# Both FFN products of a two-layer transformer made of seven half-size products instead of eight (Strassen's scheme), with a block's second product behind the next block's first

## The chip, the cores and the metric

The kernel runs on one core of one Trainium2 chip. A core has a matrix engine, TensorE (PE; its loads of stationary weights are listed apart as PEld), three engines for elementwise work, VectorE (DVE), ScalarE (ACT) and GpSimd (POOL), and queues for DMA transfers, issued here from SyncE (SP) and from POOL. Each engine works through its own instructions in order and waits on semaphores for the others. PE writes to PSUM only, which has eight banks of 512 f32 values in each of 128 partitions; DVE and ACT read PSUM, POOL works in SBUF alone. The metric is the device time of the launch in microseconds (us).

## The reference

All is f32. `x` has 4 batches of 1024 rows of 256. Two layers follow each other, an attention with 16 heads of 64 and the same FFN behind each (the reference's first attention and its second differ; neither is touched here):

```python
x = x + _L0_attn_a_ref(_layernorm(x, axis=-1), kernel, WO)
x = x + _L0_ffn_ref(_layernorm(x, axis=-1), w1, b1, w2, b2)
x = x + _L0_attn_b_ref(_layernorm(x, axis=-1), ...)
x = x + _L0_ffn_ref(_layernorm(x, axis=-1), w1, b1, w2, b2)

def _L0_ffn_ref(x, w1, b1, w2, b2):
    h = jax.nn.gelu(jnp.einsum('bse,eh->bsh', x, w1) + b1, approximate=False)
    return jnp.einsum('bsh,he->bse', h, w2) + b2
```

`w1` is 256 x 1024, `w2` is 1024 x 256.

## The kernel before

The rows of `x` stay in SBUF for the whole launch, `xs[b]` for each batch. An FFN works on eight blocks of 512 rows (`QB`), two to a batch. For a block n, `normed(n)` (L390) standardizes four tiles of 128 rows on ACT into `xn` and adds b2 to `x` on POOL. `turned(n)` (L398) transposes `xn` on PE, eight transposes of 128 x 128 into two banks of the pool `ps_mm`, and ACT copies each bank to `hT` (L156). `up(n, f)` (L403), for each of eight groups of 128 of the 1024 hidden columns, makes one tile of the first product in a bank of the pool `ps_sc`: two f32 matmuls, one for each half of the 256 inputs, with `w1` stationary and 512 rows moving. ACT applies Gelu with the bias from PSUM to `gT` (L414). `down(n, t)` (L416), for each of four tiles of 128 rows, makes the second product in a bank of `ps_mm`: eight matmuls with `gT` stationary and 256 columns of `w2` moving. After every second tile DVE adds the bank to `x` (L428), and in the last FFN SP stores those rows (L430).

The profile records an f32 matmul as two passes, each with a weight load of its own.

`ps_sc` has three buffers of two banks (in the attention they hold the scores), `ps_mm` has two of one bank. The order of instructions is written out by hand and kept (`manual_schedule`); semaphores and buffer turnover come from the framework. A new tile takes the buffer that has been free longest.

`ffn_between` (L434) weaves an FFN into the launch in three parts. `ends` are pieces for the last steps of the attention before it: block 0's `normed`, `turned` and its whole `up`, block 1's `normed` and `turned`, and the first `down(0, 0)`. `rest` is the stretch of its own: the remaining `down(0, t)`, and then for each block m from 1 the eight `up(m, f)`, `turned(m + 1)` and the four `down(m, t)`. Between the ups stand small pieces: `normed(m + 1)` after f = 1; for m = 1 after f = 2 the statistics (`measure`, two DVE instructions each) of the eight tiles of blocks 6 and 7; in the first layer after f = 3 four `measure` for layer B's norm; for m = 3 after f = 4 `finish`, which makes the factors out of the statistics (an ACT Sqrt, which needs a table load, and DVE work around it). In the first layer also `prologue`, 40 pieces that prepare the first pair of heads of layer B, one after each up for m = 4 and 5 and two for m = 6 and 7. Block 7's `down` goes behind `rest`: in the first layer into the first steps of the next attention (`last`), in the second it ends the launch.

The attention's tiles share pools with the FFN: `gT` is a buffer of pool `T`, and the pools `pT` (two buffers), `p`, `qk` and `v` stand free during `rest`, but for the prologue.

Of the kernel before, what the change touches and what calls it, by code (L numbers as in the profile page):

```python
# [15 lines left out]
P = 128  # L16
# [5 lines left out]
NF = F // P  # L22
# [17 lines left out]
def hybrid_block_kernel(  # L40
# [108 lines left out]
    def transposed(dst, src, c, affine=None):  # L149

        tr = group(TQ, P)
        for t in range(TQ):
            nc.tensor.transpose(tr[:, t, :], src[:, t, ts(c, P)], ident)  # L153
        trf = tr.rearrange("p t q -> p (t q)")
        if affine is None:
            nc.scalar.copy(dst[:, c, :], trf)  # L156
        else:
            nc.scalar.activation(
                dst[:, c, :], trf, AF.Identity,
                scale=affine[0][:, c : c + 1], bias=affine[1][:, c : c + 1],  # L160
            )
# [224 lines left out]
    def ffn(rows, store):  # L386

        xn, hT, gT, po = {}, {}, {}, {}

        def normed(n):  # L390
            b, qb = blocks[n]
            xn[n] = xnp.tile([P, TQ, D], F32, tag="xn", name="xn")
            for t in range(TQ):
                xt = xs[b][:, qb * TQ + t, :]
                standardize(xn[n][:, t, :], xt, *rows.factors(n, t)[:2])
                nc.gpsimd.tensor_add(xt, xt, b2_sb)  # L396

        def turned(n):  # L398
            hT[n] = lowp.tile([P, NC, QB], F32, tag="low", name="hT")
            for c in range(NC):  # L400
                transposed(hT[n], xn[n], c)

        def up(n, f):  # L403
            if f == 0:
                gT[n] = tp.tile([P, SENT], F32, tag="T", name="gT")[
                    :, : NF * QB
                ].rearrange("p (f q) -> p f q", f=NF)
            ph = ps_sc.tile([P, QB], F32, tag="sc", name="ph")
            for c in range(NC):
                nc.tensor.matmul(  # L410
                    ph, w1_sb[:, c, ts(f, P)], hT[n][:, c, :],
                    start=(c == 0), stop=(c == NC - 1),
                )
            nc.scalar.activation(gT[n][:, f, :], ph, AF.Gelu, bias=b1_sb[:, f : f + 1])  # L414

        def down(n, t):  # L416
            b, qb = blocks[n]
            if t % 2 == 0:
                po[n] = group(2, D)
            for f in range(NF):  # L420
                nc.tensor.matmul(  # L421
                    po[n][:, t % 2, :], gT[n][:, f, ts(t, P)], w2_sb[:, f, :],
                    start=(f == 0), stop=(f == NF - 1),
                )
            if t % 2:
                t0 = qb * TQ + t - 1
                xd = xs[b][:, t0 : t0 + 2, :]
                nc.vector.tensor_add(xd, xd, po[n])  # L428
                if store:
                    nc.sync.dma_start(ov[b, :, t0 : t0 + 2, :], xd)  # L430

        return normed, turned, up, down

    def ffn_between(rows, store, n_steps, nxt=None, prologue=(), ramp=None):  # L434

        normed, turned, up, down = ffn(rows, store)
        prologue = list(prologue)
        n = n_steps
        ends = [(n - 20 + i, lambda i=i: rows.measure(i // TQ, i % TQ)) for i in range(2 * TQ)]
        ends += [(n - 2, lambda: rows.finish[0]()), (n - 2, lambda: normed(0)), (n - 1, lambda: turned(0))]
        ends += [(n - 1 + (0, 0, 0, 1, 2, 2, 3, 3)[f], lambda f=f: up(0, f)) for f in range(NF)]
        ends += [(n, lambda: normed(1))]
        ends += [(n + 1, lambda m=m, t=t: rows.measure(m, t)) for m in range(2, 6) for t in range(TQ)]
        ends += [(n + 2, lambda: rows.finish[1]()), (n + 3, lambda: turned(1)), (n + 4, lambda: down(0, 0))]

        def rest():
            for t in range(1, TQ):
                down(0, t)
            for m in range(1, len(blocks)):
                for f in range(NF):
                    up(m, f)
                    if f == 1 and m + 1 < len(blocks):
                        normed(m + 1)
                    if f == 2 and m == 1:
                        for i in range(2 * TQ):  # L460
                            rows.measure(6 + i // TQ, i % TQ)
                    if f == 3 and nxt:
                        for t in range(TQ):
                            nxt.measure(m - 1, t) if m <= 6 else None
                    if f == 4 and m == 3:
                        rows.finish[2]()
                        if nxt:
                            nxt.finish[0]()
                    for _ in range((0, 0, 0, 0, 1, 1, 2, 2)[m]):
                        if prologue:  # L470
                            prologue.pop(0)()
                if m + 1 < len(blocks):
                    turned(m + 1)
                    for t in range(TQ):
                        down(m, t)
            while prologue:
                prologue.pop(0)()
            if nxt:
                nxt.finish[1]()
            else:  # L480
                for t in range(TQ):
                    down(len(blocks) - 1, t)

        last = [(t - 1, lambda t=t: down(len(blocks) - 1, t)) for t in range(TQ)]
        if nxt:
            last += [
                (12 + 2 * i, lambda i=i: nxt.measure(6 + i // TQ, i % TQ)) for i in range(2 * TQ)
            ] + [(30, lambda: nxt.finish[2]())]
        return ends, rest, last
# [94 lines left out]
    def layer_b(rows):  # L584
# [4 lines left out]
        def batch_b(b):  # L589
            work = []  # L590
            for qb in range(NQB):
                k = {}

                def first(t, b=b, k=k, qb=qb):
                    if t == 0:
                        if b:
                            k["x1"] = xnp.tile([P, TQ, D], F32, tag="xn", name="x1")
                        else:
                            k["x1"] = ptp.tile([P, SENT], F32, tag="pT", name="x1")[
                                :, : TQ * D  # L600
                            ].rearrange("p (t d) -> p t d", t=TQ)
                    xt = xs[b][:, qb * TQ + t, :]
                    standardize(k["x1"][:, t, :], xt, *rows.factors(NQB * b + qb, t)[:2])
                    nc.gpsimd.tensor_add(xt, xt, k["x1"][:, t, :])
# [5 lines left out]
                def turned(c, b=b, k=k, qb=qb):  # L610
                    if c == 0:
                        p, tag = (highp, f"high{qb}") if b % 2 == 0 else (lowp, "low")
                        cs[b, qb] = p.tile([P, NC, QB], F32, tag=tag, name="hc")
                    transposed(cs[b, qb], k["x1"], c, affine=(lns_sb, lnb_sb))
# [141 lines left out]
```

## Time and profile before

Three runs took 3277.23, 3277.85 and 3282.06 us, median 3277.85. The profiled execution has a span of 3281.4 us.

| what | us |
|---|---|
| span of the profiled execution | 3281.4 |
| busy: PE, DVE, ACT, POOL | 3201.6, 2531.3, 2109.0, 1958.4 |
| first product (L410), PE: 512 recorded matmuls of 512 columns | 230.2 busy |
| second product (L421), PE: 1024 recorded matmuls of 256 columns | 226.0 busy |
| weight loads of L421 | 0.190 each |
| Gelu from PSUM (L414), 128 x 512 | 0.686 each |
| add from PSUM (L428), 128 x 512 on DVE | 0.687 each |
| b2 add (L396), 128 x 256 on POOL | 0.728 each |
| first layer's FFN, `down(0, 0)` to the end of `up(7, 7)` | 1453.15 to 1676.71 |
| second layer's FFN, `down(0, 0)` to the end of the last `down` | 3061.36 to 3277.35 |

How to read the lines: a group of instructions is named by its line in the kernel, its engine, the operation, and the tiles written and read; then comes how often it ran, its busy time, the mean length of one in ns, and the idle time of the engine ahead of it with what ended it. A line of the timeline has a start, a length, and instructions that follow one another merged, with their number behind an x; a bracket gives the idle time ahead and who ended it. The chain of waits follows the last instruction back to the first, at each step to what released it.

### The profile page before, as it was taken

To read this page: it belongs to the slowest core of one execution; us is meant where nothing else is said; L and a number is where in the kernel's file an instruction comes from. 1 tells how busy PE (TensorE), PEld (TensorE's weight loads), DVE (VectorE), ACT (ScalarE), POOL (GpSimd) and SP (SyncE) were. 2 spreads that over 40 slices of the span, in tenths; PEclk is the share of its full clock that TensorE was granted. 3 is DMA by queue.
4 is the path that set the end of the run, shared out by engine and by line. 5 is a ranking of instruction groups with operands and counts; after the bars stand their busy time and mean duration, and the time that the engine had idled before them with its cause. 6 is when DMAs were issued, how large, how long until landed. Compare 5 with 4: busy or idle time off the path is not lost.

```text
span 3281.4 us, 126564 instructions
## 1 busy us (share of the span) xinstructions
PE 3201.6 (98%) x52736; PEld 2022.3 (62%) x52736; DVE 2531.3 (77%) x2386; ACT 2109.0 (64%) x4304; POOL 1958.4 (60%) x2738
## 2 busy tenths in 40 slices
PE   8999999999999999999999999999999999998999
PEld 4666666666666666666555556666656666665666
DVE  7988888888888888941049889998989999998100
ACT  5666666666666666642447777777778777777332
POOL 4544454545444445430159888998989999996110
PEclk9999999999999999999999999999999999999999
DMA  8888888888888888840029889998888899998100
GB/s 226 224 220 213 226 223 222 219 227 223 222 214 218 222 229 225 218 116 0 2 81 237 223 217 240 242 240 236 240 229 240 240 243 247 245 246 214 38 20 20
DMA packets 244697, 642.13 MB, mean 196 GB/s; under 512 B 74304, under 2 KB 102976, under 8 KB 244128
## 3 DMA queue, kind: packets, MB, share of 16 engines
q1 hardware_dynamic: 161104, 397.60, 47.6%
q0 software_dynamic: 83024, 236.44, 25.8%
q8 instruction: 419, 6.86, 0.9%
q14 instruction: 150, 1.23, 0.1%
HBM read 43.39 MB, written 4.19 MB: 15 GB/s over the span
## 4 chain that ended last, share of the span: by engine, by line
PE 78%; SPq 8%; DMA 5%; DVE 3%; ACT 3%; issue 3%; POOL 1%; DVEq 0%; POOLq 0%; ACTq 0%
PE sc L238 23%; PE mm L304 21%; PE mm L167 16%; SPq L295 7%; PE mm L421 7%; PE ph L410 7%; PE mm L176 5%; DMA pT<-T 4%; DVE T L271 1%; DVE nmax L249 1%; ACT p L251 1%; PE mm L153 1%; POOL oT L316 0%; ACT gT L414 0%; SPq L214 0%
## 5 line engine op out<-in xcount | busy, mean ns | idle before, releaser
L249 DVE TENSOR_REDUCE nmax<-sc 128x1 f32<-128x1024 f32 x1024 | 1204.5, 1218 | 226.7 <-PE sc L238 223.5
L251 ACT ACTIVATE p<-sc,nmax 128x1024 f32<-128x1024 f32 x1024 | 1145.3, 1119 | 324.0 <-DVE nmax L249 324.0
L271 DVE STREAM_TRANSPOSE T<-p 128x2176 f32<-128x2176 f32 x512 | 1247.1, 2436 | 41.0 <-DMA pT<-T 17.6
L238 PE MATMUL sc<-kT,qT 64*64 64x512 f32 x8192 | 1085.5, 599 | 16.0 <-ACT p L251 10.6
L304 PEld LDWEIGHTS mm<-pT,v 64*64 64x64 f32 x32768 | 950.3, 133 | 145.6 <-issue 103.4
L304 PE MATMUL mm<-pT,v 64*64 64x128 f32 x32768 | 984.5, 269 | 14.5 <-issue 13.5
L295 POOL DMA_DIRECT2D pT<-T x1280 | 629.6, 499 | 121.1 <-PE sc L238 56.2
L316 POOL TENSOR_TENSOR oT<-oT,pT 128x256 f32<-128x256 f32 x256 | 186.1, 727 | 718.7 <-ACT oT L314 636.3
L238 PEld LDWEIGHTS sc<-kT,qT 64*64 64x64 f32 x8192 | 333.1, 133 | 409.9 <-issue 277.1
L328 POOL TENSOR_TENSOR x<-x,got 128x512 f32<-128x512 f32 x256 | 330.9, 1293 | 27.8 <-ACT got L326 23.9
L326 ACT COPY got<-mm 128x512 f32<-128x512 f32 x256 | 150.0, 586 | 283.0 <-PE mm L167 282.9
L428 DVE TENSOR_TENSOR x<-x,mm 128x512 f32<-128x512 f32 x32 | 22.0, 687 | 367.2 <-PE mm L421 367.1
L167 PE MATMUL mm<-wo,oT 128*64 128x256 f32 x2048 | 278.4, 393 | 19.6 <-POOL oT L316 18.6
L167 PEld LDWEIGHTS mm<-wo,oT 128*64 128x64 f32 x2048 | 124.6, 136 | 266.4 <-POOL oT L316 217.4
L414 ACT ACTIVATE gT<-ph,b_sb 128x512 f32<-128x512 f32 x128 | 87.5, 686 | 301.9 <-PE ph L410 301.8
L260 ACT COPY p<-total 128x128 f32<-128x128 f32 x512 | 151.8, 296 | 195.4 <-DVE total L259 188.5
L167 PE MATMUL mm<-hT,w 128*64 128x512 f32 x1024 | 242.9, 596 | 1.0 <-ACT hT L156 1.0
L421 PE MATMUL mm<-w_sb,gT 128*128 128x256 f32 x1024 | 226.0, 381 | 6.6 <-ACT hT L156 6.6
L410 PE MATMUL ph<-hT,w_sb 128*128 128x512 f32 x512 | 230.2, 603 | 0.5 <-ACT hT L156 0.5
L421 PEld LDWEIGHTS mm<-w_sb,gT 128*128 128x128 f32 x1024 | 193.1, 190 | 39.4 <-ACT hT L156 9.4
L396 POOL TENSOR_TENSOR x<-x,b_sb 128x256 f32<-128x256 f32 x64 | 44.5, 728 | 275.6 <-ACT xn L147 275.6
L251 ACT ACTIVATION_READ_ACCUMULATOR p<-sc,nmax 128x1 f32 x1024 | 205.3, 200 | 0.0
(90 smaller groups left out, 2473.1 us busy)
## 6 DMA issues: line engine op xcount, KB each, us to landing
pT<-T SPq DMA_DIRECT2D x2688, 136.0 KB, 4.7
pT<-T POOLq DMA_DIRECT2D x1280, 136.0 KB, 4.7
turned<-kT POOLq DMA_DIRECT2D x128, 128.0 KB, 3.5
turned<-qT POOLq DMA_DIRECT2D x128, 128.0 KB, 3.3
w<-in_wqkv_a POOLq DMA_DIRECT2D x96, 128.0 KB, 6.1
wo<-in_wo_a POOLq DMA_DIRECT2D x32, 128.0 KB, 5.4
wo<-in_wo_a POOLq DMA_DIRECT2D x64, 64.0 KB, 5.5
wo<-in_wo_b SPq DMA_DIRECT2D x32, 128.0 KB, 3.6
```

What stands on the lines that cost most here:

```text
L167: nc.tensor.matmul(out[ts(j, DH)], lhsT[:, ts(j, DH)], rhs[j], start=(first and i == 0), stop=(last and i == len(parts) - 1),)
L176: nc.tensor.matmul(out[ts(j, DH)], lhsT, rhs[:, ts(j, DH)], start=(i == 0), stop=(i == len(parts) - 1),)
L238: nc.tensor.matmul(sc[s, j][ts(half, DH), ts(m, 512)], qT()[rows, ts(2 * qs + half, DH)], kT()[rows, ts(m, 512)], start=True, stop=True,)
L249: nc.vector.tensor_reduce(nmax, sc[s, j], AX.X, ALU.max, negate=True)
L251: nc.scalar.activation(probs[s][:, :NK2, ts(j, 2), :], sc.pop((s, j)).rearrange("p (k c i) -> p k c i", c=2, i=SQ), AF.Exp, bias=nmax, acc ...
L271: nc.vector.transpose(T[h][:, :, q, :, :].rearrange("p c k i -> p k c i"), probs.pop(s))
L295: engine.dma_start(pT[h][ts(c, SQ), a], T[h][ts(a, SQ), c])
L304: nc.tensor.matmul(av[h][q][ts(j ^ q, DH)], v[ts(j, DH), k, :], pT[h][ts(j, DH), :, q, k, :], start=(k == 0), stop=(k == NK2 - 1),)
L316: nc.gpsimd.tensor_mul(parts, parts, pT.pop(h)[:, :, :, NK2, :])
L328: nc.gpsimd.tensor_add(xd, xd, got)
L410: nc.tensor.matmul(ph, w1_sb[:, c, ts(f, P)], hT[n][:, c, :], start=(c == 0), stop=(c == NC - 1),)
L421: nc.tensor.matmul(po[n][:, t % 2, :], gT[n][:, f, ts(t, P)], w2_sb[:, f, :], start=(f == 0), stop=(f == NF - 1),)
```

## The change

A product C = A B, with A, B and C cut into 2 x 2 parts, is made of seven products of parts, by Winograd's form of Strassen's scheme. Four sums are made of A's parts (`four`) and four of B's (`other`). The products are P1 = A11 B11, P2 = A12 B21, P3 = S3 B22, P4 = A22 T3, P5 = S0 T0, P6 = S1 T1 and P7 = S2 T2, and with u2 = P1 + P6 and u3 = u2 + P7 the result is C11 = P1 + P2, C12 = u2 + P5 + P3, C21 = u3 + P4, C22 = u3 + P5.

For the first product A is `w1` with its 1024 columns and 256 inputs halved, and B is `hT` with the inputs and the 512 rows halved. `up(n, f)` for f = 0 to 7 becomes two calls of `up_seven`, each for two groups of 128 columns out of either half; a product there is two f32 matmuls with 256 rows moving. For the second product A is `gT` with rows and the 1024 columns halved, B is `w2`; `down_seven` makes a whole block, eight f32 matmuls a product, with 128 columns moving. The sums of the weights are made once in each FFN (`weights`), DVE those of `w1` and POOL those of `w2`; DVE makes those of `hT` (`row_sums`), DVE and POOL those of `gT` (`act_sums`).

`seven` makes the products in the order 1, 6, 2, 7, 5, 4, 3, in five banks of `ps_sc`. P2 accumulates onto P1's bank, once ACT has copied P1 out, and P3 onto P5's, once DVE has read P5. The result that can't stand in one bank goes through SBUF. After each product a hook runs the small pieces that stood between the ups, at a place from 0 to 13 (0 to 6 in a block's first seven, 7 to 13 in its second).

A block's second product goes behind the next block's first: `down_seven(m - 1)` follows `up_seven(m, 1)`, `turned(m + 1)` and `row_sums(m + 1)`. Block 0 and block 7's `down` stay as they were. Layer B's `x1` for the first batch moves from a buffer of pool `pT` to one of pool `v`.

```diff
+        def weights():
+            wc = ptp.tile([P, SENT], F32, tag="pT", name="wc")
...
+            v = nc.vector
+            work = four([s1[:, i] for i in range(4)], w1_sb[:, 0, :m], w1_sb[:, 1, :m], w1_sb[:, 0, m:], w1_sb[:, 1, m:], [v] * 4)
+            work += other([s2[:, i] for i in range(4)], lo[:, :, :P], lo[:, :, P:], hi[:, :, :P], hi[:, :, P:], [nc.gpsimd] * 4)
+            for f in work:
+                f()
+        def row_sums(n):
+            name = ("qT", "kT")[n % 2]
+            ht[n] = qkp.tile([P, S], F32, tag=name, name="ht").rearrange("p (s q) -> p s q", s=4)
+            h = hT[n]
+            for f in other(
+                [ht[n][:, i] for i in range(4)],
+                h[:, 0, :half], h[:, 0, half:], h[:, 1, :half], h[:, 1, half:], [nc.vector] * 4,
+            ):
+                f()
+        def act_sums(n):
...
+            return four(
+                [s[:, i] for i in range(4)],
+                g[:, :hf, :half], g[:, hf:, :half], g[:, :hf, half:], g[:, hf:, half:],
+                [nc.vector, nc.vector, nc.gpsimd, nc.vector],
+            )
+        def seven(product, after, hook):
+            banks = []
+            for _ in range(3):
+                t = ps_sc.tile([P, 2, 512], F32, tag="sc", name="pw")
+                banks += [t[:, 0], t[:, 1]]
+            place = {1: 0, 6: 1, 2: 0, 7: 2, 5: 4, 4: 3, 3: 4}
+            for i, k in enumerate((1, 6, 2, 7, 5, 4, 3)):
+                bank = banks[place[k]].rearrange("p (t q) -> p t q", t=2)
+                product(bank, k, k not in (2, 3))
+                after(bank, k)
+                hook(i)
+        def up_seven(n, g, hook):
...
+            def after(bank, k):
+                if k == 1:
+                    nc.scalar.copy(x1, bank)
+                elif k == 6:
+                    nc.vector.tensor_add(u2, bank, x1)
+                elif k == 2:
+                    for t in range(2):
+                        gelu(lo[:, t, :half], bank[:, t], 2 * g + t)
+                elif k == 7:
+                    nc.vector.tensor_add(u3, bank, u2)
+                elif k == 5:
+                    nc.vector.tensor_add(hi[:, :, half:], bank, u3)
+                elif k == 4:
+                    nc.vector.tensor_add(hi[:, :, :half], bank, u3)
+                    for t in range(2):
+                        gelu(hi[:, t], hi[:, t], hf + 2 * g + t)
+                else:
+                    nc.vector.tensor_add(lo[:, :, half:], bank, u2)
+                    for t in range(2):
+                        gelu(lo[:, t, half:], lo[:, t, half:], 2 * g + t)
+        def down_seven(n, hook):
...
+            def after(bank, k):
+                bank = bank[:, :, :P]
+                if k == 1:
+                    nc.scalar.copy(x1, bank)
+                elif k == 6:
+                    nc.vector.tensor_add(u2, bank, x1)
+                    nc.gpsimd.tensor_add(x12, x12, u2)
+                elif k == 2:
+                    nc.vector.tensor_add(x11, x11, bank)
+                elif k == 7:
+                    nc.vector.tensor_add(u3, bank, u2)
+                    nc.gpsimd.tensor_add(x22, x22, u3)
+                    nc.gpsimd.tensor_add(x21, x21, u3)
+                elif k == 5:
+                    nc.vector.tensor_add(x22, x22, bank)
+                elif k == 4:
+                    nc.vector.tensor_add(x21, x21, bank)
+                    if store:
+                        nc.sync.dma_start(ov[b, :, qb * TQ + 2 : qb * TQ + 4, :], xb[:, 2:])
+                else:
+                    nc.vector.tensor_add(x12, x12, bank)
+                    if store:
+                        nc.sync.dma_start(ov[b, :, qb * TQ : qb * TQ + 2, :], xb[:, :2])
...
-        ends += [(n + 2, lambda: rows.finish[1]()), (n + 3, lambda: turned(1)), (n + 4, lambda: down(0, 0))]
+        ends += [(n + 2, lambda: rows.finish[1]()), (n + 2, weights), (n + 3, lambda: turned(1))]
+        ends += [(n + 3, lambda: row_sums(1)), (n + 4, lambda: down(0, 0))]
...
+                if m + 1 <= last:
+                    when(2, lambda m=m: normed(m + 1))
+                if m == 1:
+                    for i in range(2 * TQ):
+                        when(4, lambda i=i: rows.measure(6 + i // TQ, i % TQ))
+                if nxt and m >= 2:
+                    for t in range(TQ):
+                        when(5 + t, lambda m=m, t=t: nxt.measure(m - 2, t))
+                if m == 3:
+                    when(9, lambda: rows.finish[2]())
+                    if nxt:
+                        when(9, lambda: nxt.finish[0]())
+                if m >= 2:
+                    todo = act_sums(m - 1)
+                    for i, f in zip((3, 6, 6, 9), todo):
+                        when(i, f)
                 for f in range(NF):
...
                     for _ in range((0, 0, 0, 0, 1, 1, 2, 2)[m]):
                         if prologue:
-                            prologue.pop(0)()
...
+                            when((14 * f) // NF + 1, prologue.pop(0))
...
+                up_seven(m, 0, hook)
+                up_seven(m, 1, lambda i: hook(7 + i))
+                if m + 1 <= last:
                     turned(m + 1)
-                    for t in range(TQ):
-                        down(m, t)
+                    row_sums(m + 1)
+                if m >= 2:
+                    down_seven(m - 1, lambda i: None)
```

## The prediction

> **What bounds the kernel now.** I read the page's chain of waits first, then the chain in order of time, because the change touches two stretches only (one layer's FFN at 1453 to 1696 us, the other's at 3061 to 3277 us).
>
> ```profile
> PE sc L238 23%; PE mm L304 21%; PE mm L167 16%; SPq L295 7%; PE mm L421 7%; PE ph L410 7%; PE mm L176 5%; DMA pT<-T 4%; DVE T L271 1%; DVE nmax L249 1%; ACT p L251 1%; PE mm L153 1%; POOL oT L316 0%; ACT gT L414 0%; SPq L214 0%
> ```
>
> The two products (L410 first, L421 second) hold 14% of the chain, some 460 us. In order of time the second FFN is TensorE (PE) alone:
>
> ```profile
> 3119.43 14.08 PE mm L421 x64
> 3133.51 13.75 PE ph L410 x32
> 3148.50 14.08 PE mm L421 x64
> 3162.58 13.75 PE ph L410 x32
> ```
>
> Columns: start, length, what. A block repeats every 29.07 us (3148.50 - 3119.43). A recorded matmul is one of two passes over an f32 product, so a block has 32 passes of 512 columns and 64 of 256. The windows view says who is idle beside it:
>
> ```profile
> core 0: us, PE busy (x) PEld busy (x) DVE busy (x) ACT busy (x) POOL busy (x), PEclk, DMA share, GB/s
> 3061.36:3277.35 215.99, 213.69 (x785) 144.81 (x784) 14.84 (x34) 60.01 (x97) 17.95 (x25) 1.00 0.06 19
> ```
>
> DVE works 15 of 216 us, ACT 60, POOL 18; the clock is full. So fewer passes shorten the stretch, as long as the other engines, each working strictly in its own order, never hold PE.
>
> **PE's price list** comes from the timeline between one block's two products:
>
> ```profile
> 3234.29 1.04 PE L153 MATMUL mm<-ident,xn 128*128 128x128 f32 x8
> 3234.29 0.80 PEld L153 LDWEIGHTS mm<-ident,xn 128*128 128x128 f32 x7 [0.29 <-issue]
> ...
> 3235.07 1.07 ACT L156 COPY hT<-mm 128x512 f32<-128x512 f32 x2
> 3235.70 2.46 PEld L421 LDWEIGHTS mm<-w_sb,gT 128*128 128x128 f32 x12 [0.62 <-ACT hT L156]
> 3235.71 2.64 PE L421 MATMUL mm<-w_sb,gT 128*128 128x256 f32 x11 [0.38 <-ACT hT L156]
> ```
>
> A pass of 512 columns takes 13.75 / 32 = 0.429 us. One of 256: the eleven above start over 2.64 - 0.38 (a pass's own length) - 0.10 (the first waits for its weights) = 2.16, so 0.216 each. One of 128: eight transposes start over 1.04 - 0.27 = 0.77, seven steps of 0.110. Then 29.07 = 32 x 0.429 + 64 x 0.216 + 8 x 0.110 + a rest of 0.64, in which the second product waits for a copy out of the bank it shares with the transposes.
>
> **Gain.** First product by seven: 56 passes of 256 columns, 12.10 us in place of 13.73: -1.63. Second by seven: 112 passes of 128 columns, each with its own 128-column load. The trace has no f32 stream of that shape. Lower end 0.107 a pass (a quarter of 0.429). Upper end 0.121: a load is recorded at 190 ns, and 64-column loads at L176 last 138 ns yet come 69 ns apart in one half of the array, so 69 of the 190 overlap. I take 0.110, by the transposes and by the row at 3235.70: of its eleven steps (2.46 - 0.19 = 2.27 us) ten follow the matmuls at 0.216, which leaves 0.11 for the one free step between two f32 loads. So 12.3 in place of 13.8: -1.50; to the ends, 12 blocks x 112 x (-0.003 or +0.011) = -4 or +15. The 0.64 goes, since the seven use the other six banks. A layer has 7 first and 6 second products so made (the first block and the last block's second product stay): 7 x 1.63 + 6 x 1.50 + 6 x 0.64 = 24.3; two layers: -48.6.
>
> A rule that speaks against the change: the Trainium skill, page "TensorE: Matmul & The Clock Gate", in Part 3 under "The mechanism", says that a weight load overlaps running matmuls only if it goes to another row group. Here loads and matmuls both use all rows, and loads of 190 ns beside passes at 0.216 could not fit if they took turns; the trace disagrees. By the rule a short pass would cost 0.11 + 0.107, and the sum would rise by about 12 x 112 x 0.107 = 144 us; I don't use it.
>
> **Prices on the other engines.** DVE: 512 elements out of PSUM 0.687 (L428), 1024 at L249 1.218, hence 256 at about 0.42. A 1024-element sum from SBUF has no row: between L249's 1.218 and two L428s, 1.37; I take 1.22, the same count of elements. ACT: copy of 512 0.59, of 256 0.37; gelu of 512 0.69, so of 256 0.69 - 0.21 = 0.48; with its source in SBUF, as L608 (0.51 for 256), 0.51 and 0.72. Queued ACT work overlaps by 0.1. POOL: 0.73 for 256, 1.28 for 512, so about 2.4 for 1024. From a product's last column to DVE or ACT: 0.27 (3220.55 to 3220.82, L421 to L428); back to a streaming PE: 0.16 (a copy's end, 3235.65, to a load 0.05 later, plus 0.11).
>
> A price that hides in few instructions is two engines in SBUF at once:
>
> ```profile
> 1853.74 0.17 DVE L134 TENSOR_TENSOR b_more<-b_more,b_rstd 128x8 f32<-128x8 f32 x1
> 1853.75 1.29 POOL L659 TENSOR_TENSOR qT<-qT,turned 128x512 f32<-128x512 f32 x1
> ...
> 1854.27 0.20 DVE L136 RECIPROCAL b_more<-b_more 128x8 f32<-128x8 f32 x1 [0.37 <-ACT b_more L135]
> 1854.39 0.67 DVE L137 TENSOR_TENSOR b_shift<-b_mv,b_rstd 128x8 f32<-128x8 f32 x1
> ```
>
> L137 normally takes 0.17; begun under a POOL instruction it took 0.67 and ended 0.02 after it, while the reciprocal, with one input, ran freely. I read this as: a DVE operation with two SBUF inputs waits for the running POOL one. `act_sums` and `row_sums` are of that kind; every other new DVE add has one PSUM input.
>
> **Waits that take its place.** I follow one seven of `up_seven` (0.864 us a product, order 1, 6, 2, 7, 5, 4, 3), from its first pass, in a block with `act_sums`.
> First seven. P6 ends at 1.73; ACT copies P1 out 1.13 to 1.72, and P2, into the same bank, may run at 1.88: 0.15 lost. P7 ends 3.61; u3 on DVE to 4.56. Behind it on DVE stands the first sum (hook 3). POOL's b2 adds of the next block run from 4.43, 0.7 each, so it waits to 5.13 and ends 6.35. Only then DVE reads P5 out (to 7.04), and P3, which accumulates onto P5's bank, starts at 7.20 in place of 5.34: 1.86 lost. P3 ends 8.06, DVE's adds of P4 and P3 by 7.7 and 9.0.
> Second seven, from 8.06. The sum for hook 6 wants DVE at 9.0, but POOL's own sum (2.4) runs 8.45 to 10.87: it ends 12.1. ACT, behind four gelus, copies P1 at 9.9 to 10.5; P2 starts 10.65 in place of 9.8: 0.85. DVE then does u2 (12.8), the third sum (14.0), u3 (14.7), P5 (15.4); P3 starts at 15.55 in place of 14.1: 1.45. The whole takes 16.4, of which 4.3 PE waits, so the first product is slower than its 13.73 before. `down_seven` (1.76 us a product) hides all its copies, `row_sums` too.
> Per layer: blocks 2 to 6, 5 x 4.3 = 21.5. Block 7 has no b2 adds, and POOL's sum is early: 0.15 + 1.29 + 0.86 + 0.25 = 2.55. Block 1 has eight `measure` (4.2) at hook 4, in front of P4's read on DVE (0.53 is their pace at the ramp, 16 in 8.5 us); ACT's gelus wait for that, the copy of P1 stands behind these, and PE loses 5.7. Then comes no second product, so block 2's first waits for hT's two copies and two row sums: 2.6. Block 3's `finish` puts a wait for ACT's Sqrt (table load 1.28) in front of u3: 2.2. Sum 34.6, the second layer: 34.6 - 24.3 = +10.3.
> The first layer adds four `measure` a block on DVE, about 0.95 x 6 = 5.7, and its second `finish` in block 3, 1.8. The prologue of layer B moves too, in the same order. Its weight loads issue on an empty SP queue; its eight `change` transfers issue on POOL, now behind POOL's own sum (2.4), and their rotated tiles are wanted only after the last `down_seven` (12.3), which covers that. Up to block 7's first product this layer takes 223.6 us (1453.15 to 1676.71) against 202.2 (3061.36 to 3263.52); of the 21.4 more the view of waits gives PE's waiting 6.0 - 2.3 = 3.7, so some 17 are PE work, which now falls into the gaps of blocks 5 to 7 in part, while its ACT work lengthens others: between -10 and +5, I take -5. So 34.6 + 7.5 - 5 - 24.3 = +12.8.
> At nothing: `weights` at the first ramp (POOL is idle from 3053.2 to 3059.1, its four sums need 5.2; DVE idles 10 us) - without that cover 3 to 5 us, once a layer; the stores (two a block as before, on an empty SP queue, last one behind the same last product); x1 in another pool.
>
> **Sum:** -48.6 + 34.6 x 2 + 7.5 - 5 = +23. Against the profiled 3281.4 us that is 3304.5; the runs' median is 3277.85, so 3301.
>
> **Rivals.**
> (a) POOL and DVE don't hold each other: the walk gives 14.65 in place of 16.4, five blocks, two layers: -17.7, total +5: 3283. For it: L137 is one small instruction. Against: it and L133 (ends 0.03 behind a POOL one) agree.
> (b) Faster: the sums of `act_sums` stay off the path. Then an up loses 0.15 + 0.25 + 0.92 + 0.25 = 1.57 and the layers come to 36.6 lost against 48.6: -12, 3266. It decides if DVE is free for P5 at 4.74, with u3 done at 4.56: the sum would have to fit 0.2 us, or be taken elsewhere. Against: 1.22 is the nearest row; for it: PE's prologue work fills gaps in three blocks, and my delays are taken at their full length.
> (c) More: POOL's four adds follow one another without a gap, and the first sum gets no turn among them: it starts at 7.2 in place of 5.13, 2.1 x 10 blocks = +21, 3322; with passes at 0.121, +15 and 3316; both, 3337.
> (d) The seven don't save PE time at all, loads of 190 ns one after the other: 12 x 112 x 0.08 = +107, 3408. The free step of 0.11 is against it.
>
> **Chances.** Forecast 0.47, (a) 0.12, (b) 0.20, (c) 0.18, (d) 0.03. A measurement of this kernel can tell about 0.2% from no change (6.6 us). (b) is faster; (a) lies within; the rest is slower: 0.20, 0.11, 0.69. The range goes from (b) to between (c)'s single cases and both together: 3264 to 3332; the forecast's own, with the pass from 0.107 to 0.114, 3295 to 3310.
>
> **What would show it.** Passes: 128-column matmuls of the second product about 0.110 apart. Waits: PE idle before P3 released by DVE, before P2 by ACT; two-SBUF DVE sums longer than 1.3 under POOL; a block near 29.5 us in the second layer. Wrong, if blocks come in under 28, if PE's wait before P3 is only 0.25, or if the loads pace the second product.

## The result, and the profile after

Four runs of the changed kernel took 3373.94 to 3382.33 us, median 3375.08; four of the kernel before 3277.23 to 3288.13, median 3279.95. The ratio is 1.0283 (95% interval 1.026 to 1.0305): slower by 95 us where 23 were predicted. The profiled execution has a span of 3374.2 us against 3281.4, 92.8 more.

The page of the kernel after, busy time and the chain of waits:

```profile
PE 3203.0 (95%) x53648; PEld 2091.7 (62%) x53648; DVE 2731.1 (81%) x2674; ACT 2135.2 (63%) x4400; POOL 2035.4 (60%) x2794
...
PE 68%; SPq 12%; DVE 7%; DMA 5%; ACT 4%; issue 3%; POOL 1%; DVEq 0%; ACTq 0%; POOLq 0%
PE sc L238 19%; PE mm L304 18%; PE mm L167 14%; SPq L295 11%; PE pw L482 8%; DMA pT<-T 5%; PE mm L176 4%; DVE T L271 2%; PE mm L602 2%; DVE nmax L249 2%; ACT gT L516 1%; PE ph L591 1%; ACT p L251 1%; POOL oT L316 1%; DVE gs L410 1%
```

PE is busy as long as before (3203.0 against 3201.6) in a span 92.8 longer, so PE idles about 91 us more. The FFNs hold it. The first layer's stretch, from the first pass of `down(0, 0)` to the first of the last block's `down`, went from 226.5 to 273.5 us. The second layer's, to the end of the last `down` (as the last pass has streamed, 0.16 before its recorded end), went from 215.9 to 264.0. That is +47.0 and +48.1; the attention between them took 1382.3 against 1381.8.

The chain of the kernel after in order of time, one block of the second layer (start, length, what); L482 are the passes of all sevens:

```profile
3212.99 10.08 PE pw L482 x84
3223.15 0.59 ACT u L520
3223.78 1.15 PE pw L482 x4
3225.02 0.70 DVE u L522
3225.77 2.01 PE pw L482 x8
3227.80 0.69 DVE u L527
3228.55 1.57 issue
3230.12 0.69 DVE gT L529
3230.85 1.15 PE pw L482 x4
```

Before, two lines of PE alone made up a block. Now the chain leaves PE four times within one seven: to ACT's copy of P1 (L520), to DVE's u2 (L522) and u3 (L527), and to DVE's read of P5 (L529). PE stands in the chain as a row of short pieces.

The windows of the kernel after: first the stretch of the second layer, then a steady block, then pairs of neighbours in which the clock (PEclk) is of interest later:

```profile
core 0: us, PE busy (x) PEld busy (x) DVE busy (x) ACT busy (x) POOL busy (x), PEclk, DMA share, GB/s
3106.07:3370.18 264.11, 215.31 (x1240) 180.06 (x1240) 111.36 (x176) 73.53 (x145) 49.65 (x49) 0.96 0.05 16
...
3241.69:3275.63 33.94, 27.71 (x178) 23.46 (x177) 16.38 (x24) 10.27 (x22) 8.21 (x8) 1.00 0.05 16
...
3128.29:3131.70 3.41, 0.95 (x5) 0.49 (x3) 3.21 (x13) 0.00 (x0) 0.80 (x2) 1.00 0.00 0
3131.70:3141.90 10.20, 6.35 (x14) 4.64 (x15) 2.06 (x4) 3.44 (x7) 0.00 (x0) 0.50 0.01 2
3145.39:3148.80 3.41, 1.19 (x5) 0.73 (x5) 1.52 (x4) 2.50 (x6) 0.00 (x0) 1.00 0.00 0
3148.80:3155.60 6.80, 5.95 (x13) 4.29 (x14) 0.80 (x2) 1.81 (x5) 0.41 (x1) 0.50 0.00 0
3199.99:3203.40 3.41, 0.45 (x3) 0.04 (x1) 2.10 (x5) 2.48 (x3) 0.00 (x0) 1.00 0.00 0
3203.40:3206.80 3.40, 3.17 (x8) 2.52 (x9) 1.56 (x3) 0.34 (x1) 0.00 (x0) 0.50 0.02 5
```

No engine is full in the steady block of 33.94 us (29.07 before): DVE works 16.4 of it, ACT 10.3, POOL 8.2. The engines wait for each other in turn. The view of PE's waits in that layer says for whom (waiting engine and line, releaser, then us in total, times, longest):

```profile
PE pw L482 <- ACT u L520: 18.5, 14, 5.5
PE pw L482 <- DVE u L522: 12.1, 14, 0.9
PE pw L482 <- DVE gT L529: 6.3, 6, 1.2
PE pw L482 <- ACT u L561: 3.7, 6, 0.6
PE pw L482 <- DVE u L563: 3.5, 6, 0.6
PE pw L482 <- DVE u L527: 3.2, 1, 3.2
PE pw L482 <- ACT hT L156: 1.5, 1, 1.5
```

The prediction expected the third line and a little of the first. The copy of P1 (L520) and u2 (L522) hold PE in each of 14 sevens, and the same two steps of `down_seven` (L561, L563) in each of six. Which products wait is in the timeline, the start of one block's first seven (start, length, instructions with their number; a bracket gives the idle time ahead and who ended it). Two f32 matmuls, four recorded passes, are a product; they come as P1, P6, P2, then P7 and P5 together, P4, P3:

```profile
3222.03 1.03 PE L482 MATMUL pw<-hT,w_sb 128*128 128x256 f32 x4
...
3223.15 0.58 ACT L520 COPY u<-pw 128x512 f32<-128x512 f32 x1 [12.85 <-PE pw L482]
...
3223.78 1.13 PE L482 MATMUL pw<-ht,wc 128*128 128x256 f32 x4 [0.73 <-ACT u L520]
3225.02 0.69 DVE L522 TENSOR_TENSOR u<-pw,u 128x512 f32<-128x512 f32 x1 [2.38 <-PE pw L482]
...
3225.77 1.13 PE L482 MATMUL pw<-hT,w_sb 128*128 128x256 f32 x4 [0.85 <-DVE u L522]
...
3228.39 3.76 POOL L399 TENSOR_TENSOR x<-x,b_sb 128x256 f32<-128x256 f32 x4 [9.61 <-ACT xn L147]
3228.41 1.79 DVE L409 TENSOR_TENSOR gs<-gT 128x1024 f32<-128x1024 f32 x1
...
3230.85 1.13 PE L482 MATMUL pw<-hT,wc 128*128 128x256 f32 x4 [1.18 <-DVE gT L529]
```

P6 (3223.78) begins only when ACT has copied P1, though P6 goes into another bank (1, not 0). P2 (3225.77) begins only when DVE has read P6, though P2 goes into bank 0, which ACT freed 2 us earlier. Banks 0 and 1 are one tile of the pool. P3 (3230.85) waits for the read of P5, which stands on DVE behind the first sum of `act_sums` (L409, 1.79 us beside POOL's b2 adds, L399): that is the wait that the prediction had.

### The profile page after: what moved, and what is told of

The parts are those of the page before. It is cut to its first block, busy times and chain, and to the rows that moved or that the text cites. A ratio compares the mean times of both kernels' runs of the same rounds, so it can differ in the third digit from the quotient of the medians.

```text
span 3374.2 us, 129017 instructions
## 1 busy us (share of the span) xinstructions
PE 3203.0 (95%) x53648; PEld 2091.7 (62%) x53648; DVE 2731.1 (81%) x2674; ACT 2135.2 (63%) x4400; POOL 2035.4 (60%) x2794
## 4 chain that ended last, share of the span: by engine, by line
PE 68%; SPq 12%; DVE 7%; DMA 5%; ACT 4%; issue 3%; POOL 1%; DVEq 0%; ACTq 0%; POOLq 0%
PE sc L238 19%; PE mm L304 18%; PE mm L167 14%; SPq L295 11%; PE pw L482 8%; DMA pT<-T 5%; PE mm L176 4%; DVE T L271 2%; PE mm L602 2%; DVE nmax L249 2%; ACT gT L516 1%; PE ph L591 1%; ACT p L251 1%; POOL oT L316 1%; DVE gs L410 1%
## 5 line engine op out<-in xcount | busy, mean ns | idle before, releaser
L176 PEld LDWEIGHTS mm<-w,hT 128*64 128x64 f32 x4096 | 140.9, 138 | 71.3 <-issue 69.4
L857 POOL TENSOR_TENSOR turned<-turned,sin_sb 128x512 f32<-128x512 f32 x128 | 162.7, 1271 | 0.0
L399 POOL TENSOR_TENSOR x<-x,b_sb 128x256 f32<-128x256 f32 x64 | 54.4, 880 | 166.9 <-ACT xn L147 166.9
L287 ACT COPY pT<-T 32x1088 f32<-32x1088 f32 x128 | 140.3, 1096 | 4.6 <-DMA pT<-T 1.8
L176 PE MATMUL mm<-w,hT 128*64 128x64 f32 x4096 | 140.9, 222 | 0.2 <-ACT kT L744 0.2
L167 PE MATMUL mm<-hc,w 128*64 128x512 f32 x512 | 134.0, 601 | 0.0
```

The source lines that it names most:

```text
L167: nc.tensor.matmul(out[ts(j, DH)], lhsT[:, ts(j, DH)], rhs[j], start=(first and i == 0), stop=(last and i == len(parts) - 1),)
L176: nc.tensor.matmul(out[ts(j, DH)], lhsT, rhs[:, ts(j, DH)], start=(i == 0), stop=(i == len(parts) - 1),)
L857: nc.gpsimd.tensor_mul(other, other, sin_sb[:, ts(qb, QB)])
```

## The experiments

Ten kernels ran, each beside the kernel before on the same chip; ratios are to that kernel, with a 95% interval.

**A place of its own for each product.** The theory: PE's wait for a place in PSUM goes by the tile of two banks, so P6 waits for the reader of P1. Its rival stands below with it. The edit puts products that follow each other into different tiles and leaves the order alone:

```diff
-            place = {1: 0, 6: 1, 2: 0, 7: 2, 5: 4, 4: 3, 3: 4}
+            place = {1: 0, 6: 2, 2: 0, 7: 4, 5: 3, 4: 5, 3: 3}
```

> Only the table of banks differs: P1 and P2 in the first tile, P6, P5 and P3 in the second, P7 and P4 in the third, so that no product shares a two-bank tile with the one before it. Theory T1 (PE waits go by the two-bank tile: P6 waits for the copy of P1 out of the neighbouring bank, P2 for the read of P6): P6's wait (0.9 and 1.5 in a block's two sevens, 0.8 in the second product) and P2's for u2 (about 1.0, 0.75) go; left are P2's own wait for the copy (0.15 and about 0.85) and P3's behind the sums on DVE (1.9 and up to 1.4). Block of the second layer from 33.9 to 30 or 31 us, total 3325 to 3345. Rival R1 (the queue of DVE and ACT sets the pace, the waits only change names): block above 33, total above 3362.

Measured: 3295.68 us over ten runs, ratio 1.0027 (1.0014 to 1.004). One line of bank numbers takes back some 80 of the 95 us, more than either theory had allowed for. Its timeline, the same place of a block:

```profile
3168.43 1.03 PE L482 MATMUL pw<-hT,w_sb 128*128 128x256 f32 x4
...
3169.30 1.03 PE L482 MATMUL pw<-ht,wc 128*128 128x256 f32 x4
3169.55 0.59 ACT L520 COPY u<-pw 128x512 f32<-128x512 f32 x1 [11.21 <-PE pw L482]
3170.19 1.13 PE L482 MATMUL pw<-hT,w_sb 128*128 128x256 f32 x4
...
3174.70 1.13 PE L482 MATMUL pw<-hT,wc 128*128 128x256 f32 x4 [0.60 <-DVE gT L529]
```

P6 follows P1 without a gap while ACT is copying P1, and P2 starts as soon as the copy is done (3169.55 + 0.59 = 3170.14). That is what the prediction's walk described. The view of PE's waits in the same layer, its three longest lines:

```profile
PE pw L482 <- DVE u L527: 6.3, 5, 3.2
PE pw L482 <- ACT u L520: 4.3, 7, 1.5
PE pw L482 <- DVE gT L529: 4.1, 6, 1.1
```

L522, L561 and L563 are gone from it. The steady block takes 28.51 us in place of 33.94, `down_seven` in it 12.51 in place of 14.27. The instructions and their order on each engine are the same, so the wait by tile is the cause of what went. It is set by the program, whose framework tracks readers by tile; that the chip's banks hold each other up is not shown by this. With the waits the half-speed stretches shrank too, which the expectation left out.

**The same for the second product alone**, to see whether the cause adds up: only `down_seven` gets the new places.

```diff
-        def seven(product, after, hook):
+        def seven(product, after, hook, apart=False):
...
+            if apart:
+                place = {1: 0, 6: 2, 2: 0, 7: 4, 5: 3, 4: 5, 3: 3}
...
-            seven(product, after, hook)
+            seven(product, after, hook, apart=True)
```

> The change, with the banks set apart as in e1_place in the second product alone. Theory T1: in each of 12 second products P6's wait (0.81) and P2's (0.75) and the 0.2 of reloads go, nothing else moves: 12 x 1.76 = -21 us, total 3350 to 3358 against 3375. Rival R1 (waits only change names): less than -5.

Measured: 3358.52, ratio 1.022 (1.0203 to 1.0238). The two waits of the second product (3.7 and 3.5 us a layer) are no longer in its view of waits, those of the first product are the same to 0.4 us. The ratio falls by 0.0063, some 21 us, as expected; the FFN stretches are 11.4 and 7.7 us shorter than the change's, against 2 x 7.2 of waits and the restarts behind them. The second product's part of the loss can be taken away by itself.

**The statistics out of block 1.** In block 1 the eight `measure` stand on DVE ahead of its work for the sevens, and the second wait for L520 there is 5.5 us, the longest. How much of the loss they carry, with the half-speed clock behind that wait, is the question. The edit moves them ahead of `down(0, 1)`:

```diff
+            for i in range(2 * TQ):
+                rows.measure(6 + i // TQ, i % TQ)
...
-                if m == 1:
-                    for i in range(2 * TQ):
-                        when(4, lambda i=i: rows.measure(6 + i // TQ, i % TQ))
```

> Only the eight measures of blocks 6 and 7 move, from hook 4 of block 1 to ahead of down(0, 1), where DVE idles. Theory T2 (the 5.6 us wait of block 1's second seven and the half-speed clock windows behind it hang on these): the wait falls to 1.5, the windows at 1476 to 1500 us and 3131 to 3156 us go or shrink; -8 for the waits and -8 to -14 for the clock in both layers together, total 3353 to 3360. Rival R2 (the clock falls for PE's many short waits): only the waits go, 3365 to 3368, and windows of half speed stay.

Measured: 3361.78, ratio 1.0232 (1.0215 to 1.025). In us this lies between the two expectations; the kernel before took 3287.04 beside it, 7 us more than beside the change, and by the ratios the gain is some 17 us, where the theory had 15 to 22 and the rival 7 to 10. The long wait falls from 5.5 to 1.7 us and the half-speed window of 10.2 us is gone; the 6.8 us of half speed at the start of block 2 stay, where PE waits for `hT`. The statistics cost 3.8 us of waiting a layer and about 3 of clock.

**POOL's sum on DVE.** The prediction took it that a DVE operation with two SBUF inputs waits for a running POOL operation, and let PE wait for that. Here all four sums of `act_sums` go to DVE:

```diff
-                [nc.vector, nc.vector, nc.gpsimd, nc.vector],
+                [nc.vector] * 4,
```

> The one sum of the second product's left operand that POOL makes goes to DVE too. Theory T3 (a DVE sum with two SBUF inputs waits for the running POOL instruction): the second sum, 2.36 us a piece in the profile, falls to 1.22 to 1.3, the first, which runs beside the b2 adds, stays near 1.65; the total stays within 6 us of the changed kernel (3369 to 3381), since DVE's queue is as long. Rival R3 (2.36 is what this shape costs): it stays at 2.36, and the total rises by 10 or more.

Measured: 3378.41, ratio 1.028 (1.0259 to 1.0301), the same as the change's. The groups of instructions (form, how often | busy us, mean ns | idle before), first of the changed kernel:

```profile
L410 DVE TENSOR_TENSOR gs<-gs,gT 128x1024 f32<-128x1024 f32 x12 | 28.3, 2358 | 0.0
...
L411 POOL TENSOR_TENSOR gs<-gT 128x1024 f32<-128x1024 f32 x12 | 28.2, 2354 | 3.6 <-PE pw L482 3.6
```

and of this one:

```profile
L411 DVE TENSOR_TENSOR gs<-gT 128x1024 f32<-128x1024 f32 x12 | 15.1, 1262 | 0.0
L410 DVE TENSOR_TENSOR gs<-gs,gT 128x1024 f32<-128x1024 f32 x12 | 15.1, 1256 | 0.0
```

The same sum takes 2.36 us on DVE beside POOL's, on average, and 1.26 without it, so the lock is real. In the second seven of the steady block above, the changed kernel's two sums are:

```profile
3232.12 2.35 POOL L411 TENSOR_TENSOR gs<-gT 128x1024 f32<-128x1024 f32 x1
3232.63 2.92 DVE L410 TENSOR_TENSOR gs<-gs,gT 128x1024 f32<-128x1024 f32 x1
```

DVE's began 1.84 us before POOL's ended and ends 1.08 behind it. Without POOL's sum, DVE's two sums there take 2.35 us in place of this 2.92, so DVE is free 0.6 us earlier. But u2 comes no earlier: it also needs P6, and PE holds P6 until ACT has copied P1. From the end of that copy to the start of u2 it is 1.35 us in the changed kernel and 1.29 here. So in this seven the wait by tile covers what the lock costs.

**One product alone.** First only the second product by seven, the first as before. Its `row_sums` are left out too, as nothing reads them.

```diff
-                up_seven(m, 0, hook)
-                up_seven(m, 1, lambda i: hook(7 + i))
+                for f in range(NF):
+                    up(m, f)
+                    for i in range((14 * f) // NF, (14 * f + 14) // NF):
+                        hook(i)
```

> First products as before the change (eight ups a block), second products by seven and one block later. Theory (the loss is in the first product's sevens; the second's pay about what they wait): a block of the second layer is 13.7 + 0.9 + 14.3 = 28.9 us against 29.07 before, block 2 loses about 0.8 waiting for its rows, no clock windows inside the FFN: total 3274 to 3284. Rival R5 (the second product one block later is itself costly): above 3300.

Measured: 3294.31 over ten runs, ratio 1.0023 (1.0011 to 1.0035); a total below the kernel before was expected. The block came out as expected, 28.69 us, and the two FFN stretches are 2.1 and 1.5 us shorter than before; the attention of layer B, which the edit does not touch, took 1389.6 in place of 1381.8. So the total doesn't tell the FFN's gain at this size, and the stretches have to be compared. Then only the first product by seven; `act_sums` are left out, as nothing reads them.

```diff
-                    todo = act_sums(m - 1)
-                    for i, f in zip((3, 6, 6, 9), todo):
-                        when(i, f)
...
-                    down_seven(m - 1, lambda i: None)
+                    for t in range(TQ):
+                        down(m - 1, t)
```

> First products by seven as in the change, second products as before it (eight matmuls a tile, in the banks of the transposes), one block later and without the sums of gT. Theory (the loss sits in the first product's sevens and in the copies of hT that now stand behind four gelus on ACT): a block of the second layer is 12.1 + about 5 of waits + 0.9 + 1.9 (the second product waits for hT's copy out of its bank) + 13.8 = 33.8 us, total 3365 to 3385. Rival (the sums on DVE are what makes the first product slow): block near 31, total below 3340.

Measured: 3396.56, ratio 1.0337 (1.0317 to 1.0358), slower than both products together and above what was expected. A wait that was new, of the old `down` for `hT`'s copy (L602, 8.0 us a layer in five), took the place of the sums', and the mean clock fell to 0.984. The loss sits in the first product: with its sevens alone the waits for L520 and L522 are 20.1 and 12.3 us a layer.

**A version meant to win.** The new places, P7 ahead of P2 in the order, the gelus that work in place held back until ACT has copied the next seven's P1, all four `act_sums` on DVE and in the hooks of the `down_seven` before, the statistics ahead of `down(0, 1)`:

```diff
-            place = {1: 0, 6: 1, 2: 0, 7: 2, 5: 4, 4: 3, 3: 4}
-            for i, k in enumerate((1, 6, 2, 7, 5, 4, 3)):
+            place = {1: 0, 6: 2, 2: 0, 7: 4, 5: 3, 4: 5, 3: 3}
+            for i, k in enumerate((1, 6, 7, 2, 5, 4, 3)):
...
+            def later(dst, f):
+                late.append(lambda: gelu(dst, dst, f))
...
                     nc.scalar.copy(x1, bank)
+                    flush()
...
-                        gelu(hi[:, t], hi[:, t], hf + 2 * g + t)
+                        later(hi[:, t], hf + 2 * g + t)
...
+                        for i, which in zip((2, 4, 5, 6), (2, 0, 1, 3)):
+                            when(i, lambda todo=todo, which=which: todo(which), low)
...
+                    down_seven(m - 1, lambda i, low=low: hook(i, low))
```

> All waits that the traces show are taken away at once: the order 1, 6, 7, 2, 5, 4, 3 with neighbours in different tiles; the in-place gelus of a seven behind the next seven's copy of P1 on ACT; the sums of gT, normed, the measures of layer B and the finishes moved from the first product to hooks of the second; block 6's and 7's measures ahead of down(0, 1); two of block 0's four second-product tiles behind block 1's first product, to cover its rows. Theory T1 (with the waits gone, the passes saved show): a block of the second layer 12.1 + 0.5 of waits + 0.9 + 12.5 = 26 us against 29.07 before, no half-speed windows inside the FFN, total 3235 to 3265, ratio to before 0.985 to 0.994. Rival R6 (what DVE and POOL do in the second product's stretch holds PE there, or the half-speed windows come whatever the waits): block above 28, ratio above 0.997.

Measured: 3247.41, ratio 0.9882 (0.9865 to 0.9899): 1.2% faster than the kernel before, 3.8% faster than the change. Its chain in order of time, two blocks of the second layer:

```profile
3112.59 0.87 PE mm L153 x8
3113.46 24.97 PE pw L489 x168
3138.43 0.87 PE mm L153 x8
3139.30 24.97 PE pw L489 x168
```

A block of the second layer is PE alone again, 25.85 us; the view of waits has none for a seven there, and the passes' starts leave some 0.4 us a block. The first layer kept one: P3 of one second product waits 2.1 us for DVE's read of P5 (L584), which stands behind POOL's work for layer B's prologue, and 3.4 us of half-speed clock follow, so "no half-speed windows inside the FFN" held in the second layer alone. The FFN stretches are 205.5 and 195.8 us, 41.1 shorter than before in sum; 7.2 of these come back in layer B's attention (1389.0).

**What of that is the banks.** The same version with the change's order and bank numbers. The first attempt left the hooks as they were, so that in the changed order the sum at hook 2 stood ahead of P7:

```diff
-            place = {1: 0, 6: 2, 2: 0, 7: 4, 5: 3, 4: 5, 3: 3}
-            for i, k in enumerate((1, 6, 7, 2, 5, 4, 3)):
+            place = {1: 0, 6: 1, 2: 0, 7: 2, 5: 4, 4: 3, 3: 4}
+            for i, k in enumerate((1, 6, 2, 7, 5, 4, 3)):
```

> e6_best with the order of products and the table of banks as the change has them, all else as in e6_best. Theory T1 (waits go by the two-bank tile): in each of 28 first-product sevens P6 waits 0.87 for the copy of P1 and P2 1.02 for the read of P6, in each of 12 second products 0.8 and 0.75: 28 x 1.9 + 12 x 1.55 = +72 us over e6_best, 3310 to 3328, ratio to before 1.005 to 1.013. Rival R1 (with DVE's and ACT's queues cleared such waits shrink): below 3285.

Measured: 3345.09, ratio 1.0182 (1.0166 to 1.0198). P7 of each second product takes the next block's sum S2 here in place of its own and waits for it, 9.9 us in five times a layer, which the expectation left out; so this is no measure of the banks alone. With the sum moved behind P7, and `finish` to hook 2:

```diff
-                        for i, which in zip((2, 4, 5, 6), (2, 0, 1, 3)):
+                        for i, which in zip((3, 4, 5, 6), (2, 0, 1, 3)):
```

> As e9_banks, but each sum of gT is made behind the product that last uses the one it replaces, as in e6_best (in e9_banks the hook's place let P7 wait for the next block's sum and take it). Theory T1: P6's and P2's waits alone, 28 x 1.9 + 12 x 1.45 = 53 + 17 = +70 us over e6_best's 3247, 3310 to 3325, ratio 1.006 to 1.012. Rival R1: below 3285.

Measured: 3318.33, ratio 1.0096 (1.007 to 1.0123), as expected: the bank numbers, with the order that goes with them, are worth 71 us (79 by the two FFN stretches, 242.6 and 237.2). Which part of this the order has was not measured. Its view of PE's waits in the second layer:

```profile
PE pw L489 <- DVE u L533: 12.3, 14, 1.2
PE pw L489 <- ACT u L530: 10.2, 14, 0.8
PE pw L489 <- DVE u L575: 3.5, 6, 0.6
PE pw L489 <- ACT u L572: 3.1, 6, 0.5
```

These are the copy of P1 and u2, in the first product and in the second; P3's wait, the only other one in every block of the change, is gone. With all else mended these two steps alone leave 29.1 us of waits in a layer (the sum of the four lines).

**The gelus in their old place**, in the version that won:

```diff
-                        later(hi[:, t], hf + 2 * g + t)
+                        gelu(hi[:, t], hi[:, t], hf + 2 * g + t)
...
-                        later(lo[:, t, half:], 2 * g + t)
+                        gelu(lo[:, t, half:], lo[:, t, half:], 2 * g + t)
```

> e6_best with each seven's in-place gelus left where the change has them, ahead of the next seven's copy of P1 on ACT. Theory: in a block's second seven the copy ends at 3.0 us in place of 1.7 and P2, one product later than in the change, waits 0.5; hT's copies come later too: +6 to +10 us, 3252 to 3258. Rival (the order of ACT costs nothing once P2 stands behind P7): within 3 us of e6_best.

Measured: 3256.03, ratio 0.9909 (0.9892 to 0.9925): holding them back is worth some 9 us (7.2 by the FFN stretches, 211.1 and 197.3), and without it most of the gain stays.

## Why the prediction was wrong

The direction was right; the time lies 43 us above the range's upper end. Point by point:

- **The step that failed: "P6 ends at 1.73", and "P2, into the same bank, may run at 1.88".** It let P6 follow P1 at once and asked for each bank when its reader is done. PE in fact waits for the reader of the other bank of the same tile: P6 for the copy of P1, P2 for u2 out of P6's bank. Against products that run through, P6 came 0.89 us late in the first seven of a steady block and 1.49 in the second, P2 1.02 and 1.06; the walk had 0.15 and 0.85 for P2 alone. "`down_seven` hides all its copies" fell with it: P6 0.81 and P2 0.75 late. That is 6.0 us a block where the walk had 1.0. The placing experiment mends this and nothing else, and it came out at 8.6 us over the kernel before beside it (3295.68 against 3287.04); its second layer is 9.9 us longer than before (225.8 against 215.9), where the walk said +10.3. So the walk described that kernel, not the one it was made for; in the first layer it was further off (231.7 against 226.5, +5.2, where +12.8 was said). That the second layer's sums agree is luck: a steady block there lost 28.51 - 25.85 = 2.7 us where the walk had 4.3, and 13.7 us at half speed, which the walk didn't have, made up most of the rest.
- **P3's waits** were 1.86 and 1.45; measured 1.34 and none, since PE, late already, finds P5 read. In the placing experiment P3 lost 0.77 in the first seven, and in the second P2 0.63 and P4 1.02. The walk had each such wait in the wrong size, and errors of both signs in the sum.
- **The block**: "near 29.5 us in the second layer", measured 33.94; with the places mended 28.51.
- **Passes: right.** 256 columns come 0.216 us apart, 128 columns 0.112 where 0.110 was taken, 0.2 us a block. Rival (d), loads that pace the passes, is out: 0.112 is below a load's 0.190. The 0.64 of each block went as said. The version that won shows the gain that was behind all this: 25.85 us a block against 29.07.
- **The lock of DVE and POOL: right in kind, and where it was tested without effect.** The second sum took 2.36 us beside POOL's against 1.26. Rival (a) priced its absence at -17.7; taking POOL's sum away brought nothing, 1.028 both times. The b2 adds still held the first sum there (1.63 us on average), so this half of the lock was not tested. The Trainium skill, page "SBUF — State Buffer", under "Who interferes with whom", says that a DVE instruction with two SBUF inputs contends with a GpSimd one that reads SBUF; 2.36 against 1.26 agrees.
- **Block 1's 5.7 was 5.46** (the wait for L520), and block 3's `finish`, 2.2, was 3.19; for block 2, 2.6 was taken and 1.50 went to `hT`. But the terms had no clock in them. During these three gaps PE worked so little that the clock was at half speed in the 10.2, 6.8 and 3.4 us behind each (the rows with 0.50 above); their passes took about 3, 2.7 and 1.6 us longer, some 7 a layer. Moving the statistics took the first of the three away.
- **The first layer** was to lose 2.5 us more than the second (7.5 - 5); it lost 1.1 less (47.0 against 48.1). These terms were small, and this difference is all that was measured of them.
- **Rival (b)**, faster, needed the sums off the path; with the places as they were this was not enough (1.0096). It took both, which no rival had.
- **Rival (c)**, more, is nearest in time (3337 at most) and is not what happened: the first sum got its turn behind the first of POOL's four adds (L409, 1.79 us, in the rows above), and the passes stayed at 0.112.

How the 48.1 us of the second layer divide: 38.2 go with the places (264.0 - 225.8), the half-speed clock that the longer gaps brought included; 9.9 stay, which is what the waits of P2, P3 and P4 and blocks 1 to 3 cost beyond the passes saved. What of the 38.2 is waiting and what clock was not measured one by one; the waits for L520, L522, L561 and L563 fell from 37.8 to 4.3.

## What to carry to other kernels

Before a chain of products is costed, write for each buffer tile, not for each bank, who reads it last; two outputs that different engines read at different times belong in different tiles. A stall of PE can be paid twice: the statistics of block 1 cost 3.8 us of waiting a layer and about 3 of half-speed clock behind it. And where engines hand work to each other in turn, no busy share names the cause; the view of waits, by product, does.

## What the runs showed of the hardware that was not expected

**The clock halves without PE being idle.** In the rows above, the 3.41 us ahead of each half-speed stretch have PE busy 0.95, 1.19 and 0.45 us: 28, 35 and 13%. The stretches last 3.4, 6.8 and 10.2 us, one to three times 3.41. All FFN stretches of these traces were cut into windows of that length, in step with the half-speed stretches, and the time in which PE streams was counted by the pitch of the passes. Each full-speed window that half speed followed had PE streaming for at most 0.38 of it, and those that it did not follow 0.36 or more. In the version that won, the lowest window of the second layer had 0.75 and the clock stayed full; in the first layer one had 0.31, with the 2.1 us wait in it, and 3.4 us of half speed followed. This is a reading of the traces; no run was made for it alone. The Trainium skill, page "TensorE: Matmul & The Clock Gate", Part 1 under "What's actually happening", speaks of a window of about 3.4 us that is idle; the length agrees, but here a window with a third of its time busy was enough.

**What was not touched varies by some 15 us.** The attention of layer B has the same code in all these kernels, but for `weights`, `row_sums` and `x1`'s pool against the kernel before. It took 1376.8 us (the second product's places alone) to 1392.2 (the gelus in their old place) in the profiled executions. Why was not looked into. It is larger than several of the effects sought here, so the FFN's stretches were compared beside the totals.
